# A two-layer graph network: the first layer's queries kept as three BF16 parts, with a ring of 6 lanes by 10 slots

## The chip, the cores and the metric

The kernel runs on one core of a Trainium2 chip. The metric is the device time of one execution in microseconds. Three runs gave 3413.0 (median), 3412.15 and 3419.53 us. One more execution was recorded by the profiler.

## The reference, cut to what matters

There are 6250 nodes with 256 features and 100,000 edges (`src`, `dst`, sorted by `dst`), six edge types and three node types. Two residual layers follow each other. The change is in the first, a heterogeneous graph transformer with four heads of 64:

```python
h = relu(layernorm(x))
k, q, v = typed_linear(h, ...)            # weights by node type
k_rel = einsum('nhd,rhde->rnhe', k, rel_att);  v_rel = einsum('nhd,rhde->rnhe', v, rel_msg)
att = (q[edge_dst] * k_rel[edge_type, edge_src]).sum(-1) * rel_pri[edge_type] / sqrt(64)
w = softmax of att over the edges of one (edge_dst, edge_type)
t_rel = segment_sum(w * v_rel[edge_type, edge_src], (edge_dst, edge_type))
t = mean of t_rel over the relations that are present
x = x + layernorm(typed_linear(t) * alpha + h * (1 - alpha))
```

The second layer is a graph attention layer over the same edges, with a batch norm at the end. The change doesn't touch it.

## The kernel before, in words

**Prologue (0 to about 547 us).** Two streams of work are interleaved by hand, in program order (`manual_schedule`). `sort_edges` sorts the edges by destination on VectorE. `node_stage` goes over 51 blocks of 128 nodes: it gathers rows of `x` (`take_rows`, L450), copies the weights of the block's type (`take_weights`, L458), normalizes (`norm_rows`, L488), multiplies (`keys_values`, `queries`), and scatters two tables to HBM: `hq_d` (h and q of a node) and `kv_d` (key and value of a node for each of the six relations, L418). The tile `room` is the memory of `QA` (L179), which is free until then, and serves here as scratch for the relation products.

**Queries (L913 to 921).** `load_queries` then brings q from `hq_d` to `QA`, laid out as 127 destination nodes on partitions 1 to 127 by 50 blocks, in fp32, shifted by one block. The sums of the layer are later accumulated in the same tile: the sums of block b overwrite the queries of block b-1, whose edges are done.

**Attention loop (about 547 to 1850 us).** The sorted edges lie in tiles of 128, 32 tiles to a chunk (C), 26 chunks (DENSE). Every chunk has two halves:

- `chain(c)` (L1005) scores: for a pair of tiles, it makes one-hot matrices of the destination node (`nbe`, L1030, four tiles at a time), expands q to edges by a matrix product of the one-hot and the block's queries (L1045; the block's address comes from a register), multiplies it with the gathered keys (`pr`, L1057) and reduces per head (L1060). After 16 pairs the scores are turned by TensorE (L1067) and go through segmented scans for maximum and sum (L1078, L1094, L1112, each for both passes), a reciprocal (L1151) and back, to weights `wt` (L1166).
- `bulk(c)` (L1189) sums: ScalarE weighs the gathered values (L1201), TensorE sums them per node by another one-hot (`ebn` L1179, product L1266), and VectorE adds them to the accumulators in `QA` (L1210).

Key and value of a tile come by one indirect DMA, started by GpSimd (L942), into the `ring`. The ring has NL lanes and L+1 slots of 256 fp32 per lane. Tile t uses lane t % NL; its key stands in slot s = L-1-(t // NL) % L and its value in slot s+1. So a gather overwrites, in its lane, the key of the tile NL before it, and the value of the tile NL*(L-1) before it:

```python
def gather_more():
    while gathered[0] < limit[0]:
        t = gathered[0]
        if t - NL >= scored[0] or t - NL * (L - 1) >= used[0]:
            return
        gather(ring[:, t % NL, slot(t) : slot(t) + 2, :]..., kv_d, idx[:, t, 0:1])
        gathered[0] += 1
```

It is called after each scored pair and each weighed tile. Where the ring wraps (s goes from 0 to L-1), the key of the tile before in the lane stays untouched.

**Order of the work.** `chain(c+1)` and `bulk(c)` are Python generators that a loop (L1285) advances by turns; the framework's scheduler then orders each engine's queue, so that parts of two chunks mix. A queue is worked through in order.

```python
ahead = chain(c + 1, res)
for k in range(C // 2):
    next(ahead, None)
    if k in (1, 3) or k % 2 and k > 4:
        next(todo, None)
for _ in todo:
    next(ahead, None)
```

Between two chunks a softmax that goes over the border is handed on: `move` (L1229), its product (L1234), `moved` (L1237) and an addition (L1245).

Of the kernel before, what the change touches and what calls it, by code (L numbers as in the profile page):

```python
# [24 lines left out]
def kernel(  # L25
# [97 lines left out]
    nc.gpsimd.iota(ipart_i, pattern=[[0, 1]], base=0, channel_multiplier=1)  # L123
    ipart = pers.tile([P, 1], F32, name="ipart")
    nc.vector.tensor_copy(ipart, ipart_i)
    ifree_i = pers.tile([P, P], I32, name="ifree_i")
    nc.gpsimd.iota(ifree_i, pattern=[[1, P]], base=0, channel_multiplier=0)
    ifree = pers.tile([P, P], F32, name="ifree")
    nc.vector.tensor_copy(ifree, ifree_i)
    eps_t = pers.tile([P, 1], F32, name="eps_t")  # L130
    nc.vector.memset(eps_t, EPS)

# [21 lines left out]
    def pieces(n):  # L154

        m = n - n % 16
        return [(o, e) for o, e in ((0, m), (m, n)) if e > o]
# [14 lines left out]
    def by_block(a, some):  # L172

        return a[some, :].rearrange("(b p) d -> p b d", p=BN)

    qapool = tc.tile_pool(name="qapool", bufs=1)  # L179
    QA = qapool.__enter__().tile([P, NB + 1, AV], F32, name="QA")  # L180
    room = QA.rearrange("p b a -> p (b a)")
    l0p = tc.tile_pool(name="l0p", bufs=1)
    l0c = l0p.__enter__()
# [8 lines left out]
    with ExitStack() as st:  # L192
# [168 lines left out]
        nc.vector.tensor_copy(prow_f, prow)  # L361

        RB = R * 2 * D
        nc.gpsimd.memset(room[:, 4 * RB :], 0.0)
        at_row = room[:, 2 * RB : 3 * RB + P].bitcast(BF16)[:, : NX * P].rearrange("p (x r) -> p x r", r=P)
        at_block = room[:, 3 * RB + P :].bitcast(BF16)[:, : 2 * NX * SB].rearrange("p (i x b) -> p i x b", i=2, x=NX)
        nc.vector.tensor_tensor(
# [81 lines left out]

        def take_rows(b):  # L450
            if there(b):
                xbs[b] = nwork.tile([P, D], F32, name="xb", bufs=10)
                nc.gpsimd.indirect_dma_start(
                    out=xbs[b], out_offset=None, in_=x[:, :],
                    in_offset=bass.IndirectOffsetOnAxis(ap=from_row[:, b : b + 1], axis=0),
                )

        def take_weights(b):  # L458
            if there(b):
                ws[b] = nwork.tile([P, FC, 2, D], F32, name="w_now")  # L460
# [26 lines left out]

        def norm_rows(b):  # L488
            if there(b):
                hqs[b] = nwork.tile([P, 2, D], F32, name="hq", bufs=5)  # L490
                rs = rss[b // GN]
                i = b % GN
                nc.scalar.activation(
                    hqs[b][:, 0, :], xbs.pop(b), AF.Relu, bias=rs[:, 1, i : i + 1], scale=rs[:, 0, i : i + 1]
                )
# [415 lines left out]
        nc.vector.memset(QA[:, :, D:], 0.0)  # L911

    def load_queries():  # L913
        QG = 7
        for b in range(0, NB - 1, QG):
            for o, e in pieces(BN):
                (nc.sync, nc.scalar)[b // QG % 2].dma_start(
                    QA[o + 1 : e + 1, b + 1 : b + QG + 1, :D],
                    by_block(hq_d, slice(b * BN, (b + QG) * BN))[o:e, :, D:],
                )  # L920
        nc.sync.dma_start(QA[1 : LAST + 1, NB, :D], hq_d[(NB - 1) * BN : N, D:])


    def node_by_edge(pool, c, dtype=F32):
# [24 lines left out]

    with ExitStack() as st:  # L950
        GT = 4
        NL, L = 12, 6
        cst = st.enter_context(tc.tile_pool(name="a0k", bufs=1))
        cp = st.enter_context(tc.tile_pool(name="a0c", bufs=1))
        op = st.enter_context(tc.tile_pool(name="a0o", bufs=2))
# [49 lines left out]
        def chain(c, res):  # L1005
# [15 lines left out]
            for k in range(0, C, 8):  # L1021
                t0 = c * C + k
                oh = []
                for i in range(0, 8, GT):
                    near = op.tile([P, GT, P], BF16, name="near")
                    nc.sync.dma_start(
                        near.rearrange("p g e -> p (g e)"), dap(row_d, (t0 + i) * P, [[0, P], [1, GT * P]])
                    )
                    oh.append(op.tile([P, GT, P], F32, name="nbe"))
                    nc.vector.tensor_scalar(oh[-1], near, ipart, None, op0=OP.is_equal)  # L1030
                if t0 == 0:
                    load_queries()
                _, bs = nc.values_load_multi_w_load_instructions(
                    blk[0:1, t0 // 2 : t0 // 2 + 4],
                    engines=[mybir.EngineType.PE],
                    min_val=0,
                    max_val=NB - 1,
                    skip_runtime_bounds_check_because="blk is at most NB - 1",
                )
                for j in range(0, 8, 2):  # L1040
                    t = t0 + j
                    qe = pq.tile([P, 2, D], F32, name="qe")
                    for i in range(2):
                        ordered(
                            nc.tensor.matmul(  # L1045
                                qe[:, i, :],
                                oh[j // GT][:, j % GT + i, :],
                                QA[:, 1:, :D][:, bass.ds(bs[j // 2], 1), :].rearrange("p a d -> p (a d)"),
                                start=True,
                                stop=True,  # L1050
                            ),
                            "q",
                            "sums",
                        )
                    pr = wp.tile([P, 2, H, DK], F32, name="pr")
                    lane = t % NL
                    nc.vector.tensor_tensor(  # L1057
                        pr.rearrange("p t h e -> p t (h e)"), ring[:, lane : lane + 2, slot(t), :], qe, op=OP.mult
                    )
# [127 lines left out]
        def bulk(c, w, factor):  # L1187
# [17 lines left out]
            def add(j):  # L1205

                t = c * C + j
                a = QA[:, bass.ds(state["regs"][t], 1), :].rearrange("p a d -> p (a d)")
# [10 lines left out]
            if c:  # L1219
                t = c * C // 2 - 1  # L1220
                _, (at,) = nc.values_load_multi_w_load_instructions(
                    blk[0:1, t : t + 1],
                    engines=[mybir.EngineType.PE, mybir.EngineType.DVE],
                    min_val=0,
                    max_val=NB - 1,
                    skip_runtime_bounds_check_because="blk is at most NB - 1",
                )
                move = wp.tile([P, P], F32, name="move", bufs=1)
                nc.vector.tensor_scalar(  # L1229
                    move, ifree, target[:, c : c + 1], top_row, op0=OP.is_equal, op1=OP.mult  # L1230
                )
                a = QA[:, bass.ds(at, 1), :].rearrange("p a d -> p (a d)")
# [3 lines left out]
                moved = wp.tile([P, AV], F32, name="moved", bufs=1)  # L1236
# [46 lines left out]
        for c in range(DENSE):  # L1283
            todo = bulk(c, res["w"], res.get("factor"))
            ahead = chain(c + 1, res) if c + 1 < DENSE else iter(())  # L1285
            for k in range(C // 2):
                next(ahead, None)
                if k in (1, 3) or k % 2 and k > 4:
                    next(todo, None)
            for _ in todo:  # L1290
                next(ahead, None)
            for _ in ahead:
                pass
# [6 lines left out]
                for _ in bulk(c, res["w"], res["factor"]):  # L1300
                    pass

    acc0 = QA[:, :NB, :]
# [706 lines left out]
```

## Time and profile before

| what | value |
|---|---|
| median of three runs | 3413.0 us |
| profiled execution | 3424.74 us, its span 3422.9 us |
| mean granted TensorE clock | 0.841 |
| busy: PE, weight loads, VectorE, ScalarE, GpSimd | 67%, 48%, 71%, 56%, 62% of the span |
| attention loop of layer one | about 547 to 1850 us |
| GpSimd's gathers of keys and values (L942, ring) | 832, mean 990 ns |
| score products on VectorE (L1057) | 416, mean 679 ns |
| one-hots for q (L1030) | 208, mean 489 ns |
| q products on PE (L1045) | 1664 records of 832 fp32 products, mean 421 ns |
| reciprocals (L1151), one per chunk | first at 596.7, last at 1789.6 us |

How to read the profile: times are microseconds from the start of the span, unless marked ns. PE is the matrix engine, PEld its weight loads, DVE VectorE, ACT ScalarE, POOL GpSimd, SP the engine that only starts DMAs. A row of a group has engine, operation, result<-sources, shape, count, then busy time and mean length, then the idle time just before them and what ended most of it. A row of the timeline has start and length in us, the instruction, its count when several alike are merged, and in brackets the idle time before it and its releaser. An fp32 matrix product leaves two records, a BF16 one leaves one. Releasers are inferred from semaphores: where a wait is for several, the last one by the profile is named.

### The profile page before, as it was taken

What the parts mean: (1) busy time and instruction counts of PE and PEld (TensorE: products, weight loads), DVE (VectorE), ACT (ScalarE), POOL (GpSimd) and SP (SyncE); (2) the same over time, 40 slices, a digit from 0 to 9 for tenths busy, and PEclk for the clock granted to TensorE, in tenths of its full rate; (3) what the DMA queues carried; (4) which work ended last, traced back from release to release, by engine and by line L of the source; (5) the groups of instructions that cost most, each with busy time, mean ns of one, the idle gap of its engine ahead of it and who ended that gap; (6) DMA issues with size and microseconds to landing.
All of it is one profiled execution on the core that took longest, in us unless ns stands there. A gap on an engine that the chain in (4) does not pass through costs nothing. (4 is left out here: it accounts for less than half of the span.)

```text
span 3422.9 us, 45611 instructions
## 1 busy us (share of the span) xinstructions
PE 2297.3 (67%) x9977; PEld 1630.0 (48%) x9977; DVE 2439.2 (71%) x5405; ACT 1918.9 (56%) x7430; POOL 2129.5 (62%) x2107
## 2 busy tenths in 40 slices
PE   3788784787877877777776884356555656555554
PEld 2555552555555555555544673234434434333343
DVE  7999714888888899888986995355555555555576
ACT  5655560767767777667765442244444444444446
POOL 3656545776566676666642443777777777777730
PEclk9999986999999899989998996577777777777785
DMA  3545688676566676666744773444444444444434
GB/s 99 231 191 231 194 276 226 209 215 201 177 196 205 207 212 192 196 200 205 206 128 117 203 203 118 131 126 123 114 127 129 126 126 123 127 124 127 110 88 139
DMA packets 261382, 571.48 MB, mean 167 GB/s; under 512 B 64339, under 2 KB 159849, under 8 KB 254850
## 3 DMA queue, kind: packets, MB, share of 16 engines
q0 software_dynamic: 124368, 444.93, 42.4%
q1 hardware_dynamic: 121314, 110.13, 11.8%
q10 hardware_dynamic: 15418, 13.34, 1.4%
q8 instruction: 94, 1.54, 0.2%
q14 instruction: 188, 1.54, 0.1%
HBM read 458.13 MB, written 114.06 MB: 167 GB/s over the span
## 5 line engine op out<-in xcount | busy, mean ns | idle before, releaser
L942 POOL DMA_INDIRECT ring<-kv_d,idx x832 | 823.3, 990 | 443.4 <-ACT wrows L1201 185.6
L942 POOL DMA_INDIRECT rows<-xw_d,idx x832 | 873.0, 1049 | 267.2 <-issue 203.9
L1201 ACT ACTIVATE wrows<-ring,wt 128x64 f32<-128x64 f32 x3328 | 834.3, 335 | 0.1
L1760 PE MATMUL aps<-wrows,ebn 128*128 128x264 f32 x1664 | 601.7, 502 | 303.8 <-DVE ebn L1736 150.1
L1045 PE MATMUL qe<-QA,nbe 128*128 x1664 | 475.3, 421 | 169.9 <-DVE nbe L1030 104.6
L1266 PE MATMUL aps<-wrows,ebn 128*128 128x258 f32 x1664 | 522.3, 423 | 38.1 <-ACT wrows L1201 31.4
L1760 PEld LDWEIGHTS aps<-wrows,ebn 128*128 128x128 f32 x1664 | 347.5, 236 | 387.1 <-ACT wrows L1722 336.7
L1045 PEld LDWEIGHTS qe<-QA,nbe 128*128 128x128 f32 x1664 | 337.2, 210 | 264.8 <-issue 167.5
L1722 ACT ACTIVATE wrows<-rows,ex 128x64 f32<-128x64 f32 x1664 | 434.1, 336 | 0.0
L1266 PEld LDWEIGHTS aps<-wrows,ebn 128*128 128x128 f32 x1664 | 318.4, 206 | 132.3 <-ACT wrows L1201 82.3
L1057 DVE TENSOR_TENSOR pr<-ring,qe 128x512 f32<-128x512 f32 x416 | 278.0, 679 | 141.8 <-PE qe L1045 72.9
L1579 ACT COPY asr<-rows 128x16 f32<-128x16 f32 x208 | 44.7, 216 | 571.6 <-DMA rows<-xw_d,idx 571.5
L1776 DVE TENSOR_TENSOR acc<-acc,aps 128x264 f32 x416 | 177.1, 426 | 188.3 <-PE aps L1760 174.0
L1060 DVE TENSOR_REDUCE att<-pr 128x8 f32<-128x512 f32 x416 | 268.7, 677 | 0.1
L1210 DVE SCALAR_TENSOR_TENSOR QA<-QA,same,aps 128x258 f32 x416 | 194.2, 467 | 42.1 <-PE aps L1266 38.4
L549 ACT COPY QA<-rps 128x768 f32<-128x768 f32 x204 | 164.1, 804 | 90.8 <-PE rps L548 87.8
L1381 PE MATMUL tr_ps<-wa_s,tm 128*128 128x256 f32 x600 | 148.6, 399 | 52.9 <-DVE tm L1372 52.9
L1624 DVE TENSOR_TENSOR e<-asr,ad 128x128 f32<-128x128 f32 x26 | 10.1, 389 | 216.8 <-ACT asr L1579 216.8
L1381 PEld LDWEIGHTS tr_ps<-wa_s,tm 128*128 128x128 f32 x600 | 113.6, 196 | 79.2 <-DVE tm L1372 65.0
L418 POOL DMA_INDIRECT kv_d<-QA,to_row x51 | 59.4, 1165 | 147.8 <-ACT QA L549 141.2
L1600 PEld LDWEIGHTS <-near 128*128 128x128 bf16 x832 | 96.0, 117 | 101.1 <-issue 40.8
L1736 DVE TENSOR_TENSOR ebn<-ifree,dl 128x512 f32<-128x512 f32 x208 | 142.5, 685 | 0.0
(437 smaller groups left out, 3924.7 us busy)
## 6 DMA issues: line engine op xcount, KB each, us to landing
near<-row_d SPq DMA_DIRECT2D x208, 128.0 KB
near<-row_d SPq DMA_DIRECT2D x52, 512.0 KB
ring<-kv_d,idx POOLq DMA_INDIRECT x832
rows<-xw_d,idx POOLq DMA_INDIRECT x832
keeps<-prev_d SPq DMA_DIRECT2D x416, 16.0 KB
hbuf<-hq_d SPq DMA_DIRECT2D x48, 128.0 KB
xbuf<-in_x_dram SPq DMA_DIRECT2D x48, 128.0 KB
r<-r_d SPq DMA_DIRECT2D x12, 512.0 KB
```

Source lines behind the costliest of these rows:

```text
L549: nc.scalar.copy(rel[:, :, i, 2 * c : 2 * c + 2, :].rearrange("p r h e -> p h r e"), ps)
L942: nc.gpsimd.indirect_dma_start(out=to, out_offset=None, in_=table[:, :], in_offset=bass.IndirectOffsetOnAxis(ap=index, axis=0))
L1045: nc.tensor.matmul(qe[:, i, :], oh[j // GT][:, j % GT + i, :], QA[:, 1:, :D][:, bass.ds(bs[j // 2], 1), :].rearrange("p a d -> p (a d)"), ...
L1057: nc.vector.tensor_tensor(pr.rearrange("p t h e -> p t (h e)"), ring[:, lane : lane + 2, slot(t), :], qe, op=OP.mult)
L1060: nc.vector.tensor_reduce(att[:, :, k + j : k + j + 2].rearrange("p h t -> p t h"), pr, AX.X, OP.add)
L1201: nc.scalar.activation(wv[:, j % GT, cols], v[:, cols], AF.Copy, scale=w[:, h, j : j + 1])
L1210: nc.vector.scalar_tensor_tensor(a, a, same[:, t : t + 1], sums.pop(j), op0=OP.mult, op1=OP.add),
L1266: nc.tensor.matmul(sums[j - j % 2], hot[j // GT][:, j % GT, :], wvs[j // GT][:, j % GT, :], start=(j % 2 == 0), stop=(j % 2 == 1),)
L1381: nc.tensor.matmul(tr, m[:, t, c, :], wa_s[:, t, c, :], start=(t == 0 and c == 0), stop=(t == T - 1 and c == FC - 1),)
L1722: nc.scalar.activation(wv[:, part, h, :DK], rows[:, part, h, :DK], AF.Copy, scale=ex[:, 0, h, g * GT + part : g * GT + part + 1],)
L1760: nc.tensor.matmul(sums[t - t % 2], oh[:, t % GT, :], wv[:, t % GT].rearrange("p h e -> p (h e)"), start=(t % 2 == 0), stop=(t % 2 == 1),)
L1776: nc.vector.tensor_tensor(a, a, sums.pop(t).rearrange("p (h e) -> p h e", h=H), op=OP.add)
```

## The change

Six edits go together.

1. `QA` grows from 258 to 386 fp32 per block. `load_queries` loads q in groups of 4 blocks (13 loads in place of 7, all of 128 partitions but the first and the last) and splits it: hi = BF16 of q, mid = BF16 of q - hi, lo = the rest. The three sum up to q exactly.
2. The one-hots `nbe` become BF16, and q is expanded by three BF16 products that add up in one fp32 bank.
3. The ring has NL, L = 6, 10 in place of 12, 6: 66 places of 256 fp32 instead of 84.
4. The loop that interleaves the halves takes a step of `bulk` at k > 1 (14 of 16) in place of k in (1, 3) and odd k > 4 (8 of 16).
5. The prologue's rows, weights and normalized rows (`xb`, `w_now`, `hq`) get fixed places in `room` in place of tiles of a pool.
6. `move` and `moved` share a buffer of `pr`; a small index tile is freed early.

```diff
-    QA = qapool.__enter__().tile([P, NB + 1, AV], F32, name="QA")
+    QW = AV + D // 2
+    QA = qapool.__enter__().tile([P, NB + 1, QW], F32, name="QA")
+    Q3 = QA.rearrange("p b a -> p (b a)").bitcast(BF16).rearrange("p (b a) -> p b a", a=2 * QW)
+    Q3 = [Q3[:, :, o : o + D] for o in (0, D, 2 * AV)]
...
-                xbs[b] = nwork.tile([P, D], F32, name="xb", bufs=10)
+                xbs[b] = room[:, X0 + b % 10 * D : X0 + (b % 10 + 1) * D]
...
-                ws[b] = nwork.tile([P, FC, 2, D], F32, name="w_now")
+                o = 4 * RB + b % 2 * FC * 2 * D
+                ws[b] = room[:, o : o + FC * 2 * D].rearrange("p (c i d) -> p c i d", c=FC, i=2)
...
-                hqs[b] = nwork.tile([P, 2, D], F32, name="hq", bufs=5)
+                o = H0 + b % 5 * 2 * D
+                hqs[b] = room[:, o : o + 2 * D].rearrange("p (i d) -> p i d", i=2)
...
-    def load_queries():
-        QG = 7
-        for b in range(0, NB - 1, QG):
-            for o, e in pieces(BN):
-                (nc.sync, nc.scalar)[b // QG % 2].dma_start(
-                    QA[o + 1 : e + 1, b + 1 : b + QG + 1, :D],
-                    by_block(hq_d, slice(b * BN, (b + QG) * BN))[o:e, :, D:],
-                )
+    def load_queries(pool):
+        QG = 4
+        for i, b in enumerate(range(0, NB, QG)):
+            n = min(QG, NB - b)
+            full = n if b + n < NB else n - 1
+            eng = (nc.sync, nc.scalar)[i % 2]
+            q = QA[:, b + 1 : b + n + 1, QW - D :]
+            if b:
+                eng.dma_start(
+                    q[:, :full, :],
+                    dap(hq_d, (b * BN - 1) * 2 * D + D, [[2 * D, P], [BN * 2 * D, full], [1, D]]),
+                )
...
+            hi, mid, lo = (a[:, b + 1 : b + n + 1, :] for a in Q3)
+            rest = pool.tile([P, GT, AV], F32, name="wrows")[:, :n, :D]
+            nc.scalar.copy(hi, q)
+            nc.vector.tensor_tensor(rest, q, hi, op=OP.subtract)
+            nc.scalar.copy(mid, rest)
+            nc.vector.tensor_tensor(lo, rest, mid, op=OP.subtract)
...
-        NL, L = 12, 6
+        NL, L = 6, 10
...
-                    oh.append(op.tile([P, GT, P], F32, name="nbe"))
+                    oh.append(op.tile([P, GT, P], BF16, name="nbe"))
...
-                        ordered(
-                            nc.tensor.matmul(
-                                qe[:, i, :],
-                                oh[j // GT][:, j % GT + i, :],
-                                QA[:, 1:, :D][:, bass.ds(bs[j // 2], 1), :].rearrange("p a d -> p (a d)"),
-                                start=True,
-                                stop=True,
-                            ),
+                        for n, q in enumerate(Q3):
+                            ordered(
+                                nc.tensor.matmul(
+                                    qe[:, i, :],
+                                    oh[j // GT][:, j % GT + i, :],
+                                    q[:, 1:, :][:, bass.ds(bs[j // 2], 1), :].rearrange("p a d -> p (a d)"),
+                                    start=(n == 0),
+                                    stop=(n == 2),
+                                ),
...
-                move = wp.tile([P, P], F32, name="move", bufs=1)
+                hand = wp.tile([P, 2, H, DK], F32, name="pr").rearrange("p t h e -> p (t h e)")
+                move, moved = hand[:, AV : AV + P], hand[:, :AV]
...
-                if k in (1, 3) or k % 2 and k > 4:
+                if k > 1:
                     next(todo, None)
```

More of the change, by code (lines that the diff above doesn't have):

```diff
@@ L125 @@
     nc.vector.tensor_copy(ipart, ipart_i)
-    ifree_i = pers.tile([P, P], I32, name="ifree_i")
-    nc.gpsimd.iota(ifree_i, pattern=[[1, P]], base=0, channel_multiplier=0)
     ifree = pers.tile([P, P], F32, name="ifree")
-    nc.vector.tensor_copy(ifree, ifree_i)
+    with tc.tile_pool(name="early", bufs=1) as early:
+        ifree_i = early.tile([P, P], I32, name="ifree_i")
+        nc.gpsimd.iota(ifree_i, pattern=[[1, P]], base=0, channel_multiplier=0)
+        nc.vector.tensor_copy(ifree, ifree_i)
     eps_t = pers.tile([P, 1], F32, name="eps_t")
@@ L363 @@
         RB = R * 2 * D
-        nc.gpsimd.memset(room[:, 4 * RB :], 0.0)
+        X0 = 4 * RB + 2 * FC * 2 * D
+        H0 = X0 + 10 * D
+        Z0 = H0 + 5 * 2 * D
+        assert Z0 <= (NB + 1) * QW
+        if Z0 < (NB + 1) * QW:
+            nc.gpsimd.memset(room[:, Z0:], 0.0)
         at_row = room[:, 2 * RB : 3 * RB + P].bitcast(BF16)[:, : NX * P].rearrange("p (x r) -> p x r", r=P)
@@ L909 @@
         nc.vector.tensor_scalar(nalpha, alpha, -1.0, 1.0, op0=OP.mult, op1=OP.add)
-        nc.vector.memset(QA[:, :, D:], 0.0)
-    def load_queries():
-        QG = 7
-        for b in range(0, NB - 1, QG):
-            for o, e in pieces(BN):
-                (nc.sync, nc.scalar)[b // QG % 2].dma_start(
-                    QA[o + 1 : e + 1, b + 1 : b + QG + 1, :D],
-                    by_block(hq_d, slice(b * BN, (b + QG) * BN))[o:e, :, D:],
-                )
-        nc.sync.dma_start(QA[1 : LAST + 1, NB, :D], hq_d[(NB - 1) * BN : N, D:])
+    def load_queries(pool):
[9 more added lines that the diff above has]
+                    dap(hq_d, (b * BN - 1) * 2 * D + D, [[2 * D, P], [BN * 2 * D, full], [1, D]]),
+                )
+            else:
+                nc.vector.memset(q[0:1, :, :], 0.0)
+                for o, e in pieces(BN):
+                    eng.dma_start(
+                        q[o + 1 : e + 1, :full, :], by_block(hq_d, slice(b * BN, (b + full) * BN))[o:e, :, D:]
+                    )
+            if full < n:
+                nc.vector.memset(q[:, full, :], 0.0)
+                eng.dma_start(q[1 : LAST + 1, full, :], hq_d[(NB - 1) * BN : N, D:])
+            hi, mid, lo = (a[:, b + 1 : b + n + 1, :] for a in Q3)
[4 more added lines that the diff above has]
+            nc.vector.tensor_tensor(lo, rest, mid, op=OP.subtract)
+        nc.vector.memset(QA[:, :, D:AV], 0.0)
     def node_by_edge(pool, c, dtype=F32):
@@ L1028, in chain @@
                     )
-                    oh.append(op.tile([P, GT, P], F32, name="nbe"))
+                    oh.append(op.tile([P, GT, P], BF16, name="nbe"))
                     nc.vector.tensor_scalar(oh[-1], near, ipart, None, op0=OP.is_equal)
                 if t0 == 0:
-                    load_queries()
+                    load_queries(wp)
                 _, bs = nc.values_load_multi_w_load_instructions(
@@ L1043, in chain @@
                     for i in range(2):
-                        ordered(
-                            nc.tensor.matmul(
-                                qe[:, i, :],
-                                oh[j // GT][:, j % GT + i, :],
-                                QA[:, 1:, :D][:, bass.ds(bs[j // 2], 1), :].rearrange("p a d -> p (a d)"),
-                                start=True,
-                                stop=True,
-                            ),
-                            "q",
-                            "sums",
-                        )
+                        for n, q in enumerate(Q3):
[7 more added lines that the diff above has]
+                                ),
+                                "q",
+                                "sums",
+                            )
                     pr = wp.tile([P, 2, H, DK], F32, name="pr")
@@ L1207, in add @@
                 t = c * C + j
-                a = QA[:, bass.ds(state["regs"][t], 1), :].rearrange("p a d -> p (a d)")
+                a = QA[:, bass.ds(state["regs"][t], 1), :AV].rearrange("p a d -> p (a d)")
                 ordered(
@@ L1231, in bulk @@
                 )
-                a = QA[:, bass.ds(at, 1), :].rearrange("p a d -> p (a d)")
+                a = QA[:, bass.ds(at, 1), :AV].rearrange("p a d -> p (a d)")
                 ps = pp.tile([P, AV], F32, name="aps")
@@ L1235, in bulk @@
                 yield
-                moved = wp.tile([P, AV], F32, name="moved", bufs=1)
                 nc.vector.tensor_tensor(
@@ L1301 @@
                     pass
-    acc0 = QA[:, :NB, :]
+    acc0 = QA[:, :NB, :AV]
     adst = pers.tile([P, NB, 3, 2 * H], BF16, name="adst")
```

## The prediction

> **What bounds the kernel now.** I read the stretches of the span first, to find the stage that the change touches. The first layer's attention loop (26 chunks of 32 edge tiles) fills 547 to 1850 us; its steady part is the row below. Columns: length, busy time of PE, PE weight loads, DVE, ACT and POOL (with instruction counts), granted clock, DMA share, GB/s.
>
> ```profile
> 597.00:1790.00 1193.00, 924.33 (x3562) 664.24 (x3560) 1046.07 (x2326) 861.16 (x3783) 776.16 (x784) 0.91 0.67 198
> ```
>
> 25 chunks in 1193 us are 47.7 us each. DVE is busy 88% of it, PE 77%, ACT 72%, POOL 65%. But POOL does nothing here but start gathers, and its groups on the page and its rows in the timeline show that 65% understates it:
>
> ```profile
> L942 POOL DMA_INDIRECT ring<-kv_d,idx x832 | 823.3, 990 | 443.4 <-ACT wrows L1201 185.6
> L1045 PE MATMUL qe<-QA,nbe 128*128 x1664 | 475.3, 421 | 169.9 <-DVE nbe L1030 104.6
> L1057 DVE TENSOR_TENSOR pr<-ring,qe 128x512 f32<-128x512 f32 x416 | 278.0, 679 | 141.8 <-PE qe L1045 72.9
> ```
>
> A gather is 0.95 us and then 0.30 us of issue, so 1.25 us back to back; with the mean of 0.99 it is 1.28. Thirty-two of them are 41 us of a 47.7 us chunk: POOL has 6 to 7 us to spare, about as little as DVE. Who waits for whom (700 to 1700 us) says the same; the first row is the score product waiting for a gather to land:
>
> ```profile
> DVE pr L1057 <- DMA ring<-kv_d,idx: 43.9, 39, 4.2
> DVE pr L1057 <- PE qe L1045: 33.5, 63, 1.0
> ```
>
> Then one chunk in the timeline, DVE's score products (first two, last, first two of the next chunk), and POOL's gathers 12, 16 and 31 of that chunk (counted: the n-th gather is tile n, the n-th product is tiles 2n and 2n+1).
>
> ```profile
> 1023.06 1.27 DVE L1057 TENSOR_TENSOR pr<-ring,qe 128x512 f32<-128x512 f32 x2
> ...
> 1056.83 0.69 DVE L1057 TENSOR_TENSOR pr<-ring,qe 128x512 f32<-128x512 f32 x1 [0.71 <-DMA ring<-kv_d,idx]
> ...
> 1070.94 1.27 DVE L1057 TENSOR_TENSOR pr<-ring,qe 128x512 f32<-128x512 f32 x2
> ```
>
> ```profile
> 1024.47 0.95 POOL L942 DMA_INDIRECT ring<-kv_d,idx  x1 [3.61 <-ACT wrows L1201]
> ...
> 1032.14 0.95 POOL L942 DMA_INDIRECT ring<-kv_d,idx  x1 [2.97 <-ACT wrows L1201]
> ...
> 1052.40 0.95 POOL L942 DMA_INDIRECT ring<-kv_d,idx  x1 [0.30 <-issue]
> ```
>
> The reader is to see a loop. The first product ends at 1023.7 and 0.73 us later gather 12 starts, though the row names another releaser: with 12 lanes, gather t overwrites the key of tile t-12. From there to the end of gather 31 (1053.35) POOL needs 29.6 us, 20 gathers and some 4 us of stalls; 3.5 us later it has landed and the last product starts, having waited 0.71 us for it. From that product to the next chunk's first lie 14.1 us (the softmax scans), and 0.67 us to its end. 29.6 + 3.5 + 14.1 + 0.7 = 47.9 us. So the chunk is a burst of scoring paced by gathers and a tail paced by DVE, and the lanes decide how many gathers fit under the tail: 12 of 32.
>
> **The ring (L 12,6 to 6,10).** With 6 lanes only 6 gathers can run ahead of the scoring; 26 must come after the chunk's first product. The order of the changed program on DVE is as before in what matters: product 0 and 1 stand in the tail after the second row scans, 14 products follow the reciprocal, the tail holds much the same work (I add up 12.3 us from its last product to the next first, against 12.8 before), so I keep 14.1. The sum from the end of product 0: 0.73 to the first gather; 26 x 1.28 = 33.3, less 0.3 after the last; 0.7 of idle after the first two, because product 1 ends 3.2 us after product 0 (scans, a reduction and sums stand between) and releases the next two at 3.9 where POOL is free at 3.2; landing 3.4; tail 14.1 and 0.7. That is 51.9 us. Products that arrive late also hold up, on their in-order engine, the reductions, one-hots and sums queued behind them: between 0 and 3 us per chunk, nothing in the trace isolates it; the new queue has three places where 1 to 2.6 us of other work stands between two products while a release allows 1.4, so I take 1.3. Together 53.2, or +5.5 on 47.7. Over 25 chunks: +137 us. DVE is then busy some 41 of 53 us, and idle in the burst.
>
> A second loop lies close: product k releases the gathers of pair k+3, so 0.67 + 0.73 + 2.5 + landing for three pairs. With 3.4 us of landing it gives 2.43 us per pair, just under POOL's 2.5. Landings in this chunk ran from 2.9 to 4.9 us; at 4.9 the loop gives 2.9 and the chunk costs 5 us more.
>
> Value slots: a gather may now overwrite the value of 54 tiles back, not 60. In the new order that value is weighed some 13 us before it is needed, so it costs nothing; without that cover, a chunk would wait for ACT, 1.05 us per tile.
>
> In the first chunk (547 to 597) no sums run; its products end 29 us after the first. There 26 gathers instead of 20 follow: 6 x 1.25 = +7 us.
>
> **The three products on PE.** Removed: 1664 fp32 records. Eight of them take 1.89 us, the last 0.38 of it its own length, so a pitch of 0.216 us, 359 us in all. Added: 2496 BF16 products with a weight load and a register instruction each. The nearest row is layer two's BF16 product with a register address:
>
> ```profile
> 1053.88 1.89 PE L1045 MATMUL qe<-QA,nbe 128*128 x8
> ```
>
> ```profile
> 2162.91 0.80 PE L1600 MATMUL ad<-adst,near 128*128 x6 [0.71 <-ACT a L1633]
> ```
>
> Pitch (0.80 - 0.18)/5 = 0.124 us, for 24 columns; ours have 256. Lower end 0.124 (310 us, -2 us per chunk), upper end the 0.216 of an fp32 record of that width (539 us, +7 per chunk, PE then at 44 of 53 us). I take 0.13, nearer the row of the same type: -35 us of PE. Either way DVE and POOL are later, so 0 on the path.
>
> **The one-hots (L1030).** 208 at 0.489 us; in BF16 both ways the row of L1588 (2048 elements in 0.755) puts them between 0.19 and 0.45; I take 0.34. DVE gains 8 x 0.15 = 1.2 us per chunk, but in the burst, where it now idles: 0 on the path, at most -2.4 per chunk if DVE still were the limit. Here the Trainium skill has a rule (SBUF — State Buffer, section "Who interferes with whom"): a tensor_scalar in a two-port mode takes the port pair that it shares with GpSimd, and the other fully blocks for its whole length. The row: beside two one-hots at 1041.35 us the gathers took 1.02 and 1.07 us, not 0.95, so 0.1 each. By the rule the shorter one-hot would give POOL back 8 x 0.15 = 1.2 us per chunk, 30 us in all (3533); by the row 0.2 us. I follow the row and count 0.
>
> **Pacing (k > 1).** 14 steps of sums beside the scoring instead of 8. ACT weighs 24 tiles before the scores turn, so it isn't late in the tail, and PE's six sums before the turning cost the tail up to 1 us, against one shorter row there. 0.
>
> **The queries' loads and split.** Same 6.4 MB from 501 to about 546 us, in 4-block groups. Per group two ACT copies of 1024 elements (L549: 768 in 0.804, so 1.07 us) and two DVE subtractions (L1954: 1024 in 1.22): 28 us of ACT and 32 of DVE, both idle then, beside the loads; exposed are the last group's 4.6 us and up to 4 us of copies queued before it on ACT, whose last load also stands behind copies. Against it, six gathers fewer (1.5 MB at 217 GB/s, 7 us) precede the loads. Between -3 and +12; I take +5. The prologue's buffers move into a room that is otherwise unused then; its order of instructions is unchanged, the node steps keep their 6.2 us: 0.
>
> **Sum.** 137 + 7 + 5 = 149 us. The profiled execution took 3424.7 us (span 3422.9), 0.3% over the median of 3413.0; on it 3574, as median about 3562.
>
> **Rivals.**
> - DVE is the bound, as its 88% suggests, and the lead of 6 suffices because the burst is longer: per chunk -1.2 to -2.4 us from the one-hots. For it: 72.9 us of waits for q go too. Against: the last product waits for its gather already with 12 lanes. 25 x -1.8 + 5 = -40: 3373. It decides if the gap from gather 12's release to the last product stays under 33 us.
> - The shorter lead is half hidden, because the rounds in which the ring wraps (every 60 tiles) need no release and because sums fill the waits: +1.5 per chunk, 38 + 12: 3463.
> - Landing takes 4.9 us throughout: +10.5 per chunk, 262 + 12: 3687.
>
> **Chances.** The main case (3490 to 3640) 0.72, DVE-bound 0.13, half hidden 0.08, long landing 0.07. The range 3435 to 3640 holds the main case and most of the half-hidden one. A measurement here tells 0.2% (7 us) from no change; faster 0.13, within 0.02, slower 0.85.
>
> **What would show it.** Right: chunk period near 53 us; POOL idle 10 us or more in every tail and back to back in the burst; the score product's wait for gathers at several hundred us in place of some 60; its wait for q small; DVE's share in the loop under 80%; L1045's successors at 0.12 to 0.14 us pitch. Wrong: periods under 48 us, a gather released before the product three pairs ahead of it, or a tail that shrinks by several us because the scans no longer meet sums.

## The result, and the profile after

| | before | after |
|---|---|---|
| median of the runs, us | 3412.6 (3401.1 to 3419.5) | 3580.1 (3573.9 to 3583.8) |
| ratio, 95% interval | 1 | 1.0493 (1.0468 to 1.0519) |
| span of the profiled execution, us | 3422.9 | 3575.0 |
| first score product starts at, us | 549.5 | 551.6 |
| end of the first product, chunk 1 to chunk 25: 24 periods of | 48.00 | 53.77 |
| end of the last product of chunk 25, us | 1770.7 | 1921.5 |
| from there to the end of the span, us | 1652.2 | 1653.5 |

The change is slower by 152.1 us of span. The rows say where: 2.1 us before the first score product, 3.0 us more up to the end of chunk 1's first product, 24 x 5.77 = 138.5 us in the steady chunks, 7.2 us in the last chunk's own scoring, 1.3 us in all that follows. So the loop holds it, at the same place of every chunk: from the end of a chunk's first product to the start of its last (the burst) 39.2 us pass instead of 33.5, and from there to the end of the next first product (the tail) 14.6 us (14.5 before).

First the loop's stretch in the windows of the changed kernel, columns as in the prediction:

```profile
603.00:1893.00 1290.00, 913.94 (x4231) 606.52 (x4229) 993.84 (x2259) 845.53 (x3683) 743.50 (x767) 0.86 0.60 179
```

DVE is busy 77% of it, PE 71%, POOL 58%: every share has fallen, so no engine has become the bound by its own work; they wait. For what, the costliest groups of the page and DVE's waits from 700 to 1700 us show (columns of the latter: us in total, times, the longest):

```profile
L973 POOL DMA_INDIRECT ring<-kv_d,idx x832 | 805.8, 968 | 613.7 <-ACT wrows L1233 148.4
L1077 PE MATMUL qe<-QA,nbe 128*128 x2496 | 430.9, 310 | 255.8 <-DVE pr L1089 132.0
L1089 DVE TENSOR_TENSOR pr<-ring,qe 128x512 f32<-128x512 f32 x416 | 282.7, 680 | 279.4 <-DMA ring<-kv_d,idx 207.5
```

```profile
DVE pr L1089 <- DMA ring<-kv_d,idx: 152.8, 103, 4.5
DVE pr L1089 <- PE qe L1077: 36.8, 39, 2.2
```

POOL's idle time before gathers has grown from 443 to 614 us, though it is the pace-maker; the score product now waits 152.8 us for gathers, 3.5 times what it did. One chunk of the timeline shows both. DVE's score products of chunk 18 (first two, then the last two) and the first of chunk 19:

```profile
1504.11 0.66 DVE L1089 TENSOR_TENSOR pr<-ring,qe 128x512 f32<-128x512 f32 x1
1506.94 0.62 DVE L1089 TENSOR_TENSOR pr<-ring,qe 128x512 f32<-128x512 f32 x1
...
1540.80 0.68 DVE L1089 TENSOR_TENSOR pr<-ring,qe 128x512 f32<-128x512 f32 x1
1545.36 0.69 DVE L1089 TENSOR_TENSOR pr<-ring,qe 128x512 f32<-128x512 f32 x1 [2.30 <-DMA ring<-kv_d,idx]
1561.07 0.66 DVE L1089 TENSOR_TENSOR pr<-ring,qe 128x512 f32<-128x512 f32 x1
```

And POOL's gathers 6, 29, 30 of chunk 18 and, by their count, 5 and 6 of chunk 19:

```profile
1505.51 0.95 POOL L973 DMA_INDIRECT ring<-kv_d,idx  x1 [10.01 <-ACT wrows L1228]
...
1534.50 0.94 POOL L973 DMA_INDIRECT ring<-kv_d,idx  x1 [0.30 <-issue]
1539.40 0.94 POOL L973 DMA_INDIRECT ring<-kv_d,idx  x1 [3.96 <-ACT wrows L1233]
...
1548.13 0.94 POOL L973 DMA_INDIRECT ring<-kv_d,idx  x1 [0.30 <-DVE ebn L1211]
1562.47 0.94 POOL L973 DMA_INDIRECT ring<-kv_d,idx  x1 [13.40 <-ACT wrows L1228]
```

The reader is to see that gather 6 starts 0.74 us after the chunk's first product ends (1504.77), whatever releaser the row names; that gathers then run at 1.25 us each, 24 in a row with one step of 1.54; that gather 30 waits for product 12 (ended 1538.66); and that POOL, having fetched six ahead, stands still for 13.4 us of the tail, in which before it fetched twelve. It starts again 0.74 us after the next first product ends.

### The profile page after: what moved, and what is told of

It reads as the page before. It is cut to its first block, busy times and chain, and to the rows that moved or that the text cites. A ratio compares the mean times of both kernels' runs of the same rounds, so it can differ in the third digit from the quotient of the medians.

```text
span 3575.0 us, 48919 instructions
## 1 busy us (share of the span) xinstructions
PE 2314.4 (65%) x10809; PEld 1585.7 (44%) x10809; DVE 2451.3 (69%) x5433; ACT 1949.4 (55%) x7456; POOL 2114.1 (59%) x2107
## 3 DMA queue, kind: packets, MB, share of 16 engines
q14 instruction: 188, 1.54, 0.1%
## 5 line engine op out<-in xcount | busy, mean ns | idle before, releaser
L973 POOL DMA_INDIRECT ring<-kv_d,idx x832 | 805.8, 968 | 613.7 <-ACT wrows L1233 148.4
L1298 PE MATMUL aps<-wrows,ebn 128*128 128x258 f32 x1664 | 550.7, 458 | 140.9 <-DVE ebn L1211 79.5
L1077 PE MATMUL qe<-QA,nbe 128*128 x2496 | 430.9, 310 | 255.8 <-DVE pr L1089 132.0
L1792 PEld LDWEIGHTS aps<-wrows,ebn 128*128 128x128 f32 x1664 | 348.9, 236 | 387.4 <-ACT wrows L1754 302.3
L1298 PEld LDWEIGHTS aps<-wrows,ebn 128*128 128x128 f32 x1664 | 332.4, 224 | 269.8 <-ACT wrows L1233 145.2
L1077 PEld LDWEIGHTS <-nbe 128*128 128x128 bf16 x2496 | 272.9, 110 | 397.6 <-issue 226.4
L1611 ACT COPY asr<-rows 128x16 f32<-128x16 f32 x208 | 44.8, 216 | 584.2 <-DMA rows<-xw_d,idx 584.0
L1092 DVE TENSOR_REDUCE att<-pr 128x8 f32<-128x512 f32 x416 | 275.9, 677 | 0.3
L1228 ACT CAST wrows<-start 128x8 f32<-128x8 bf16 x208 | 39.5, 191 | 301.1 <-PE aps L1298 297.8
```

What stands on the lines that cost most here:

```text
L973: nc.gpsimd.indirect_dma_start(out=to, out_offset=None, in_=table[:, :], in_offset=bass.IndirectOffsetOnAxis(ap=index, axis=0))
L1077: nc.tensor.matmul(qe[:, i, :], oh[j // GT][:, j % GT + i, :], q[:, 1:, :][:, bass.ds(bs[j // 2], 1), :].rearrange("p a d -> p (a d)"), st ...
L1092: nc.vector.tensor_reduce(att[:, :, k + j : k + j + 2].rearrange("p h t -> p t h"), pr, AX.X, OP.add)
L1298: nc.tensor.matmul(sums[j - j % 2], hot[j // GT][:, j % GT, :], wvs[j // GT][:, j % GT, :], start=(j % 2 == 0), stop=(j % 2 == 1),)
L1792: nc.tensor.matmul(sums[t - t % 2], oh[:, t % GT, :], wv[:, t % GT].rearrange("p h e -> p (h e)"), start=(t % 2 == 0), stop=(t % 2 == 1),)
```

## The experiments

The theory is the prediction's: the lanes set how many gathers must follow the first product, and that sets the chunk. The rivals: the BF16 arithmetic carries part of the loss; the pacing does; DVE bounds the chunk. Periods below are means over chunks 1 to 25 of the profiled run, measured as in the table. "Before" was 3417 to 3424 us in these runs, and ratios are to it.

**The ring alone, without and with the pacing.** The kernel before, with

```
-        NL, L = 12, 6
+        NL, L = 6, 10
```

and in the second run also

```
-                if k in (1, 3) or k % 2 and k > 4:
+                if k > 1:
```

> The kernel before with one edit, the ring at 6 lanes of 10 places. Theory (26 gathers instead of 20 must follow the chunk's first product, 1.25 to 1.28 us each): nearly the whole loss is here, a chunk of 53 to 55 us and 3413 + 25 x 5.8 + 7 = about 3560 us (3540 to 3590). Rival (the three BF16 products, the split and the one-hots carry a good part of the loss, and the ring the rest): well under 3540; 3490 if they share it evenly. Rival (DVE bounds the chunk, lanes hardly matter): 3413 to 3430.

> The kernel before with the ring at 6 lanes of 10 places and with the change's pacing (k > 1), so that every key is fetched ahead of the product that reads it (in the run with the ring alone 73 of 832 tiles were scored from the key that lay in their place before). Theory (the lanes are nearly the whole loss, pacing costs nothing): 3555 us (3535 to 3585), chunk 53 to 54.5 us. Rival (the BF16 edits carry part of it): under 3530. Rival (the pacing does): this run is slower than the theory says, and the run with the pacing alone is too.

Measured: 3567.4 us, 1.043 (1.038 to 1.048), period 54.17; and with the pacing 3557.5 us, 1.041 (1.038 to 1.043), period 53.31. In the first run a value's place is overwritten 54 tiles later instead of 60, while the old pacing weighs too late for that: counted in the program's order, 73 of the 832 tiles are scored ahead of their own gather, from an older key, so that run leaves their waits out. The second has them all and is the one to go by. The ring, with the pacing that it needs, makes 4.1 of the 4.9 points of the loss. Its trace has the same sign as after, where the score product waits 184.0 us for gathers in the loop (603 to 1893 us); the row is that of its own loop, 590 to 1860 us:

```profile
DVE pr L1057 <- DMA ring<-kv_d,idx: 178.9, 113, 4.1
```

**The pacing alone.** 

> The kernel before with the pacing alone (k > 1). Theory: no change, 3413 us within 25 (1 us per chunk either way: six more steps of sums beside the scoring, which hold up products, and six fewer in the tail, which hold up scans). Rival (sums ahead of the score products on the in-order DVE delay the releases): 3440 to 3480.

Measured: 3428.0 us against 3423.8, 1.0011 (0.9999 to 1.0024), period 47.89 against 48.00. No change that this can tell; the rival falls.

**More and fewer lanes in the changed kernel.** Three runs: `NL, L = 10, 6`, the same with `if k > 0:` for `if k > 1:`, and `NL, L = 4, 15`.

> The changed kernel with 10 lanes of 6 places instead of 6 of 10. Theory: 22 gathers follow the first product instead of 26, so 4 x 1.25 to 1.28 = 5 us less per chunk, period about 48.8, and 3580 - 25 x 5 = 3455 us (3430 to 3480). Rival (value slots: 50 tiles back instead of 54 make the gathers wait for the weighing): 3500 or more. Rival (the BF16 edits carry half the loss): 3580 less half of 125, so 3515.

> The changed kernel with 10 lanes of 6 places and sums from the second step on (k > 0), so that the last tile of each chunk is fetched ahead of its product, which the run with 10 lanes and k > 1 did not have (24 tiles were scored from an older key, and the chunk's last product did not wait for the last gather). Theory: the earlier run got one gather per chunk too cheaply, 1.25 us x 24 = 30 us: 3428 + 30 = 3458 us (3440 to 3475). Rival (that gather lay off the path): 3428 within 8.

> The changed kernel with 4 lanes of 15 places. If only the count of gathers behind the first product matters, 2 x 1.28 = 2.6 us more per chunk: 3645 us. Theory, with the second loop of the prediction: a product now releases the pair two ahead, so two pairs take 0.67 + 0.73 + 2.5 + about 3.1 of landing = 7.0 us, 3.5 per pair instead of 2.5; 15 pairs make 52.5 between the first and the last product and with 15 of tail a chunk is 67 us, +13.5 x 25 = +340: 3915 us (3850 to 3980). Rival (DVE bounds): under 3600.

Ten lanes: 3428.2 us, 1.0034 (1.0021 to 1.0048), period 48.12, which is better than the theory allowed. The reason is the one that the second run was made for: in the first the last tile of 24 chunks is scored from an older key, and its product starts a median of 3.1 us after the last gather starts, where the gathers whose landing the trace of the change holds (104 of 832) took 3.3 us at least; in the second run it is 4.3. The second: 3454.8 us, 1.0094 (1.0074 to 1.0113), period 48.49: 5.28 us less per chunk than with 6 lanes, where 4 gathers of 1.25 to 1.28 make 5.0 to 5.1. The second run is slower by 20 us, not by 30, and half of that is a later first product (557.0 against 547.2 us), which stands ahead of all that the pacing orders; the missing gather itself was worth 24 x 0.37 = 9 us at most, within the scatter and near the rival that put it off the path. That the run fell within the theory's range is then chance. Both runs keep a value for only 50 tiles, fewer than the change's 54, and the chunk still gained: this speaks against the value slots as what the change pays for.

Four lanes: 3717.5 us, 1.086 (1.082 to 1.090), period 58.80. Neither sum fits. The second loop is there: from the start of one product to the next pass 3.50 us on average (52.4 us from the first to the last; 3.5 worked out), against 2.66 with 6 lanes. But the tail did not stay. The products, the scans of the row (L1110, L1144) and the reciprocal in the timeline of that run, from the last product of a chunk on:

```profile
1240.86 0.69 DVE L1089 TENSOR_TENSOR pr<-ring,qe 128x512 f32<-128x512 f32 x1 [1.98 <-DMA ring<-kv_d,idx]
1243.65 0.73 DVE L1110 TENSOR_TENSOR_SCAN one<-keeps,a 128x128 f32<-128x128 f32 x2
1246.55 0.85 DVE L1144 TENSOR_TENSOR_SCAN both<-keeps,col,a 128x128 f32<-128x128 f32 x2
1247.32 0.66 DVE L1089 TENSOR_TENSOR pr<-ring,qe 128x512 f32<-128x512 f32 x1
1249.42 0.68 DVE L1089 TENSOR_TENSOR pr<-ring,qe 128x512 f32<-128x512 f32 x1
1250.09 0.72 DVE L1110 TENSOR_TENSOR_SCAN one<-keeps_s,ex 128x128 f32<-128x128 f32 x2
1253.94 0.69 DVE L1089 TENSOR_TENSOR pr<-ring,qe 128x512 f32<-128x512 f32 x1 [1.36 <-DMA ring<-kv_d,idx]
1254.68 0.84 DVE L1144 TENSOR_TENSOR_SCAN both<-keeps_s,col,ex 128x128 f32<-128x128 f32 x2
1257.42 0.93 DVE L1183 RECIPROCAL w<-den 128x128 f32<-128x128 f32 x1
```

With 6 lanes the next chunk's first product stands after all scans; here the scheduler puts three products among them, and the time from the last product to the end of the next first is 7.0 us, not 14.6. The order is an outcome of the ring's size too, and my sum had taken it as given.

**The BF16 part alone, at 12 lanes.** The kernel before with q split into `hi` and `mid` in the fp32's own room, `op.tile([P, GT, P], BF16, name="nbe")`, and

```
+    Q3 = [hi, mid, mid]
...
+                        for n, q in enumerate(Q3):
```

> The kernel before with the BF16 part of the change alone: q split, BF16 one-hots, three BF16 products, ring and pacing left as they were. To keep the room of 12 lanes only the first two BF16 parts are stored, and the third product takes the second part once more, so q comes out slightly wrong; the counts of products and loads are those of the change (the split has a copy more and a subtraction less). Theory (these edits lie off the path): 3370 to 3420 us, the one-hots' 1.2 us per chunk and the vanished waits for q giving back at most 40 us, the split taking about 5. Rival (they carry part of the loss): 3440 or more; 3490 if half.

Measured: 3440.6 us, 1.0058 (1.0036 to 1.0080). A miss by 20 us, and the trace says where: the first product starts at 585.8 us instead of 549.5, because my split worked on one group at a time (both its buffers are taken from one pool of two) and outlasted the loads: DVE stands idle 3.0 us per group for ACT's copies, 4.2 us pass from group to group. The number is the rival's, the place is not: the loop lost nothing, 47.06 us per chunk against 48.00 (chunks scatter by some 2 us, so a mean of 24 by about 0.5, and the difference of two means by 0.7: too near to call it a gain). At 12 lanes the BF16 arithmetic is no loss in the loop; how much a split costs depends on how it is laid beside the loads.

**More lanes than before.** The kernel before with `NL, L = 14, 5` and `k > 1`:

> The kernel before with 14 lanes of 5 places (the same room, values 56 tiles back) and the change's pacing. Theory (gathers behind the first product set the burst): 18 instead of 20, 2.5 us less per chunk until another engine is next; DVE is busy 42 us of a chunk, so the period goes to about 45.5: 3413 - 25 x 2.3 - 2 = 3350 us (3340 to 3390). Rival (DVE's order bounds the chunk before 45 us): 3400 to 3420.

Measured: 3346.3 us, 0.977 (0.975 to 0.979), period 44.83. Faster than both kernels, from the same room. The loop's windows and DVE's waits (640 to 1640 us):

```profile
640.00:1640.00 1000.00, 804.85 (x3233) 574.19 (x3232) 940.97 (x2104) 780.22 (x3426) 725.83 (x720) 0.96 0.72 216
```

```profile
DVE pr L1057 <- PE qe L1045: 27.6, 73, 1.6
...
DVE pr L1057 <- DMA ring<-kv_d,idx: 6.1, 6, 2.0
```

DVE is busy 94%; gathers are hardly waited for. Here DVE is next in line, as the first rival had it for the 12-lane kernel. That lighter work on DVE would now shorten the chunk is not shown by this; the next runs ask it.

**BF16 where DVE is busiest.** That kernel with BF16 one-hots and q in two parts (`Q3 = [hi, mid]`), then with 16 lanes, then with a third product:

> The kernel before with 14 lanes of 5 places, k > 1, and q kept in two BF16 parts in the fp32's own room (off by at most 2 to the -17 of its size; two products, BF16 one-hots, a split of one subtraction and three copies per group). Theory: with 14 lanes DVE is the bound (94% busy in that run's loop, 44.8 us per chunk, of which 1.2 us waits for q), so what was worth nothing at 6 lanes counts here: 8 one-hots x 0.15 us and the waits for q, 1.2 to 2.4 us per chunk, less 5 to 10 us of split: 0.967 of before, 3310 us at 3424 (3285 to 3335), chunk 42.5 to 43.7. Rival (the BF16 edits are worth nothing at any number of lanes): 0.977 plus the split, 3350.

> As the run with two parts and 14 lanes, with 16 lanes of 5 places (the small buffers' room makes up for it). Theory (DVE bounds at 14 lanes, gathers are waited for 6 us in 1000): no more than 10 us better than 14 lanes. Rival (gathers still set the burst at 14): 2.5 us per chunk, 60 us better.

> As the run with two parts and 14 lanes, with a third product that takes the second part once more (q slightly wrong), so that PE has the change's 2496 products. Theory (PE has room beside a DVE that is 94% busy): within 10 us of the run with two products. Rival (832 more products, 4.2 us of PE per chunk, hold up the scores once the gathers don't): 20 to 100 us slower than it.

Measured: 3346.8 us, 0.978 (0.976 to 0.979), period 44.90; with 16 lanes 3340.1, 0.977 (0.975 to 0.978), 44.60; with three products 3356.1, 0.981 (0.979 to 0.983), 45.46. The lanes go as the theory said, at most 7 us left at 16; the third product costs 9 us, within the 10 allowed. The intervals of these three runs overlap, so neither difference is certain. But the gain of 35 us from the one-hots and shorter waits did not come. Of it the split takes some 10 us (first product at 554.6 us, 543.4 without), but the chunk stayed as well. DVE's busy share fell to 92%, as it should, and its wait for q took the place, the first row of its waits in the two-part run at 14 lanes:

```profile
DVE pr L1082 <- PE qe L1070: 53.1, 94, 1.7
```

53.1 us instead of 27.6 (640 to 1640 us in both), though PE has less to do. PE's sums in that run last 437 ns each (700 to 1600 us), 406 without the BF16 part, and the granted clock is 0.89 there and 0.96 without. Whether the waits come from the slower clock or from the other order of PE's queue these runs do not separate.

**The third part left out of the change.**

```
-            nc.vector.tensor_tensor(lo, rest, mid, op=OP.subtract)
...
-                        for n, q in enumerate(Q3):
+                        for n, q in enumerate(Q3[:2]):
```

> The changed kernel with the third part left out: neither computed (one of two subtractions per group of the split, 13 of 1.18 us) nor multiplied (832 of 2496 products, 32 per chunk x 0.13 us); q is off by at most 2 to the -17. Theory (PE's products lie off the path, the split's DVE work is exposed in the prologue): the first score product comes 10 to 15 us sooner, the chunk stays at 53.8 within 0.5: 1.0455 of before (1.041 to 1.049). Rival (the products on PE delay scores or sums): up to 32 x 0.13 = 4.2 us per chunk less, 1.015 to 1.03 of before.

Measured: 3608.6 us, 1.055 (1.053 to 1.057): slower than the change itself. The first product came 5.8 us sooner (545.8; 10 to 15 were expected), but the chunk is 55.33 us, 1.56 more, of which 1.15 lie in the tail and 0.41 in the burst. The windows of 700 to 1600 us and PE's fp32 sums in them, the change first:

```profile
700.00:1600.00 900.00, 636.67 (x2926) 424.32 (x2926) 685.28 (x1549) 579.61 (x2522) 518.42 (x535) 0.85 0.60 179
```

```profile
L1298 PE MATMUL aps<-wrows,ebn 128*128 128x258 f32 x1056 | 353.2, 465 | 85.5 <-DVE ebn L1211 55.8 <-ACT wrows L1233 15.3 <-DVE QA L1242 10.5
```

then the run without the third part:

```profile
700.00:1600.00 900.00, 611.15 (x2334) 392.43 (x2333) 673.16 (x1512) 569.05 (x2479) 503.70 (x518) 0.77 0.58 172
```

```profile
L1297 PE MATMUL aps<-wrows,ebn 128*128 128x258 f32 x1038 | 394.5, 511 | 96.3 <-DVE QA L1241 64.8 <-DVE ebn L1210 20.5 <-ACT wrows L1232 4.4
```

PE has less to do, is granted 0.77 instead of 0.85, and each sum takes 511 ns instead of 465: 10% more, as the clocks' ratio (0.85/0.77 = 1.10). The rival (less PE work, shorter chunk) is refuted, and so is my "nothing". That the slower clock is what lengthened the chunk fits, but the scheduler's order of the products differs as well in this run, so it is not shown.

## Why the prediction was right, step by step

The direction, the mechanism and nearly the size held: 149 us forecast, 152 in the span. That the total came so close is in part luck. The prediction's sum for the chunk leaves out a term of its own list: 0.73 + 33.3 - 0.3 + 0.7 + 3.4 + 14.1 + 0.7 make 52.6 us, not 51.9; with the 1.3 for late products 53.9 and not 53.2, and the whole 167 us and not 149. The measured 53.77 fits the full list. What the slip hid is that the chunk before is 48.0 us by the products' ends and not 47.7, that the first chunk gave 3.0 us and not 7, and what the items below say.

- *26 gathers behind the first product instead of 20.* Right, and shown by undoing it: in the changed kernel the period falls from 53.8 us at 6 lanes to 48.5 at 10; in the kernel before with the change's pacing it is 53.3 at 6, 47.9 at 12 and 44.8 at 14; with two BF16 parts 44.9 at 14 and no clear gain at 16 (44.6). So a lane was worth 1.3 us from 6 to 10, 0.9 from 6 to 12 and 1.5 from 12 to 14, where a gather back to back takes 1.25. The count is not always 26 and 20: where the ring wraps, more run ahead. Counted in the traces, 24.5 gathers a chunk start behind the first product's end after and 19.9 before (chunks 1 to 24); 4.7 of 1.25 us are 5.8 us, the measured 5.77. The same quotient in the other pairs lies between 1.0 us (6 to 12 lanes) and 2.8 (12 to 14), so one issue interval is the right size and no exact price.
- *The terms of the sum.* Release 0.73 us: 0.74 in chunk 18. Landing 3.4: a median of 3.1 from the last gather's end to the last product. Tail and first product 14.8: 14.6. Sum up to the last product 37.8 + 1.3 = 39.1: 39.2 in the mean. Inside it two things cancel. The place where the ring wraps needs no release; when that falls into the tail, 8 to 12 gathers run ahead, in 7 of the 22 chunks from the third on. These take 37.3 us, the others 39.8. I had given the wraps to a rival and not to the main sum, and what late products hold up, 1.3, is 2.0 in the chunks without a wrap (39.8 less 37.8).
- *First chunk +7.* 36.4 us from first to last product instead of 29.3: +7.1. Of that 4.1 us came back in its tail, which has no sums.
- *The three products: 0.13 us of pitch, 0 on the path.* The pitch (from the start of one to the start of the next) is right, six in 0.90 us with 0.27 for the last, so 0.126:

```profile
1504.82 0.90 PE L1077 MATMUL qe<-QA,nbe 128*128 x6
```

  The "0 on the path" is not quite: after has 53.77 us per chunk, the same ring with fp32 q 53.31 (0.46 x 24 = 11 us, about the size of the chunk-to-chunk scatter). What the step lacked is PE's clock: 0.90 from 700 to 1600 us with fp32 products on the same ring, 0.85 after, and an fp32 sum takes 434 and 465 ns.
- *One-hots: 0.34 us, 0 on the path.* A mean of 0.355 in the loop (0.501 with fp32 and 6 lanes). On the shared port the row was nearer than the rule: a gather lasts 0.970 us after and 0.983 with fp32 one-hots (700 to 1600 us), 0.4 us for 32, where the rule would have given 1.2 and my row 0.2. Whether these one-hots run in a two-port mode at all, no run here shows.
- *Pacing 0.* Shown: 1.0011. What I did not see is that the pacing is no free choice here: with the old one, 54 places are too few in this program.
- *Queries: +5 us.* The first product came 2.1 us later. But the prologue ahead of it ends at different times: its last scatter into `kv_d` is over at 500.6 us before, at 498.6 after and at 494.5 in the 6-lane kernel with fp32 q (one profile each). Counted from there, the first product starts 48.9, 53.0 and 40.9 us later. So the fewer gathers ahead of the loads are worth 8.0 us (7 forecast), the exposed split costs 12.1 (12 forecast), and the net is +4.1; 2.0 of it was given back by the earlier end of the prologue, which the forecast had put at 0 and which no run isolates. The windows from 520 to 550 us of the changed kernel show that it outlasts the loads:

```profile
520.00:530.00 10.00, 0.00 (x0) 0.00 (x0) 6.99 (x6) 9.78 (x12) 0.00 (x0) 0.50 0.73 229
530.00:540.00 10.00, 0.00 (x0) 0.00 (x0) 9.26 (x8) 6.31 (x8) 0.00 (x0) 0.50 0.16 53
540.00:550.00 10.00, 0.00 (x0) 0.10 (x1) 8.52 (x10) 4.24 (x7) 0.00 (x0) 0.50 0.00 0
```

The DMA share (last but one) is gone by 540, while DVE (third busy column) subtracts to the end: 26 of 1.18 us are 30.7 us, they start at 512.6 when the first loads have landed, and end at 549.1. I had hung the exposure on the last group; it was the throughput of DVE, so the size was right for another reason.

- *What would show it.* POOL back to back in the burst and DVE at 77%: as said. POOL idle for 10 us or more at a stretch holds in 13 of 24 tails, not in every one; where the ring wraps the stretch is shorter. The score product's wait for q was to be small; over the whole run it fell from 72.9 to 52.5 us only. The wait for gathers is 184 us in the loop, three times before's and not the "several hundred" that I wrote; the rest of DVE's 296 idle us stands before other instructions.

DVE as the bound fell for this kernel. At 14 lanes it is busy 94%, but lighter one-hots gained nothing there, so that it bounds the chunk even then is not shown. That landing takes 4.9 us throughout fell as well (3.1).

Left open: what the BF16 arithmetic would be worth with lanes enough, since in the 14-lane runs clock and order changed together; why two lanes more than 12 gave more than their gathers; and what a change of the value slots alone would do, though with fewer tiles (50) and more lanes the chunk gained.

## What to carry to other kernels

Where transfers are paced by buffers coming free, count how many can start before the next burst opens: each lane was worth 0.9 to 1.5 us per round here, about one issue interval (1.25 us), though POOL and DVE both looked under-used in the kernel after. Before paying buffers for a cheaper operation, ask whether that operation's engine ends any wait last, and try the opposite trade: two lanes more, from the same room, gave 2.3%. And a smaller buffer may change the scheduler's order and the program order that is safe, so cost it together with the pacing that it needs.

## What the runs showed of the hardware

TensorE's granted clock went down where it was less busy, and it fell without a long pause. In the 14-lane run with two parts no pause of PE and its weight loads was over 2.63 us (700 to 1600 us), yet the clock went to half. Two stretches of its windows, PE's busy time first:

```profile
1100.00:1104.00 4.00, 1.54 (x10) 0.77 (x8) 4.00 (x8) 4.00 (x18) 3.09 (x4) 0.91 0.87 253
1104.00:1108.00 4.00, 3.43 (x8) 2.66 (x9) 3.53 (x8) 0.35 (x2) 3.08 (x4) 0.50 0.67 208
```

4 us at 38% busy are followed by 4 us at half clock. The Trainium skill (TensorE: Matmul & The Clock Gate, section "Why this matters for your kernels") asks for no idle gaps over about 3 us to keep the clock; here that was met and was not enough, so the measurement decides: a busy share below a half over some microseconds did it too. In all traces of this case the granted clock has only the values 1.0 and 0.5, in stretches of whole multiples of 3.41 us. In the changed kernel (640 to 1640 us), 56 such steps at full clock were followed by one at half: PE was busy a median of 41% of them, and 61% at most; the 150 followed by full clock had 48% at least. Over 700 to 1600 us the mean clock was 0.96, 0.91, 0.85 and 0.77 with PE busy 80%, 78%, 71% and 68% (14 lanes with fp32; before; after; after without the third part), and an fp32 sum took 406, 424, 465 and 511 ns. The sums' growth is the clock's: at full clock a sum took a median of 381 ns in each of these four runs, at half about 650, and 4%, 11%, 25% and 42% of the sums stood at half. The mean busy share is not all of it: the run with 16 lanes had 0.91 at 69%, so how the pauses lie may count. I had not expected that taking work from TensorE can make its other work slower; the sums became longer in each pair of runs that differ in the products (12 lanes 424 to 437 ns; 14 lanes 406 to 421 with three and 437 with two; 6 lanes 434 to 465 with three and 511 with two). At 12 lanes the mean clock is 0.91 with and without, so that pair shows it least.
